# Two-layer graph attention with expert routing: pairwise routing, split slot search and early weights in the change

## The chip, the cores and the metric

The kernel runs on one core of one Trainium2 chip. The metric is the device time of one execution in microseconds (us), as the median of several runs. Below, PE is the matrix engine (TensorE), DVE the vector engine (VectorE), ACT the scalar engine (ScalarE), POOL is GpSimd, and SP is the engine whose queue issues most transfers between memory (HBM) and the on-chip SBUF. PSUM is the memory that matrix products land in.

## What is computed

`x` has 2708 rows of 256 float32 numbers and `adj` is a 2708 x 2708 matrix of zeros and ones. Two layers follow each other. Each one adds a graph attention to `x` and then a mixture of experts:

```python
x = x + _L0_gnn_ref(_layernorm(x), adj, L0_gnn_W, L0_gnn_a)
x = x + _L0_ffn_ref(_layernorm(x)[None], Wg, bg, W1, b1, W2, b2)[0]       # 8 experts, 256 -> 1024 -> 256, gelu
x = x + _L1_gnn_ref(_layernorm(x), adj, 1, W_gcn, W_att, a_att)
x = x + _L1_ffn_ref(_layernorm(x)[None], gate_w, gate_b, w1, b1, w2, b2, gamma, beta)[0]  # 16 experts, 256 -> 512 -> 256, relu
```

In both mixtures a row picks the two experts with the highest gate logits. The softmax over these two logits gives their weights. The output of an expert is `act(x @ W1[e] + b1[e]) @ W2[e] + b2[e]`, and a row's result is the weighted sum of its two experts. The second mixture adds its input and normalises the sum with `gamma` and `beta`.

## The kernel before

The 2708 rows are 22 tiles of 128 rows (the last holds 20), one row per SBUF partition. Instructions are written in program order. A scheduling layer then sets the order on each engine, and each engine works through its own list strictly in that order, waiting at an instruction whose input is not there yet. The stages follow one another, and only their edges overlap:

1. **Attention 0** (the loop over `pairs` of two tiles, 0 to 333 us). For each pair, `weigh` (ACT L722, DVE L725) makes the scores against each of the 22 tiles and `gather` (PE L735) sums them up. The work that `beside` lists is spread between: for the pair before, the layer norm, `Router.turn` (writes the rows to memory as `rows_d`, transposes them) and `Router.gate` (PE L341, DVE L364: the logits).
2. **Routing 0** (start of `experts`, L404 onward). From the logits of all tiles at once, DVE finds the two experts of each row as a one-hot tile `hot` (L429 to L441). Matrix products with a triangle of ones and with ones (L451, L455) count how many rows before each row have the same expert. A scan (L461) adds up over the tiles. Every (row, choice) gets a slot in the list sorted by expert. The slots are cut into blocks of 128 that belong to one expert each (at most NB = 50 blocks in layer 0, 58 in layer 1). Then the list is inverted: for each of 44 groups (22 tiles, 2 choices) the tile `in_block` (L523) says which place in a block a row takes and `which` (L513 to L518) says in which block, and the product of the two (L525) leaves the row's number at its place. This gives `comes` (which row to fetch) and `goes` (where to write the result). `whose` is the expert of a block. Biases are spread over blocks (L555). The weighted `b2` is added to every tile (the loop with L567 transpose, L569 copy, L571 product, L572 add). Only then does `gates_scope.close()` give the memory to the pool that holds the expert weights.
3. **Experts 0** (the loop over 50 blocks). SP loads 1 MB of W1 (L584) and 1 MB of W2 (L586) per block, with three buffers each. POOL gathers 128 rows (L589). PE transposes them (L336), computes the hidden part (L601, with ACT L603 behind it) and the output of the block before (L611). DVE copies it out (L614) and POOL scatters it into `outs_d` (L615).
4. **Combine 0 with projection 1** (`ready1`, then L640 onward). `ready1` loads the weights of the second attention (W_gcn, W_att, a_att) into a pool of its own on the freed memory, and multiplies them into `w1x` (L846, L852). Then each tile's two results are read back as `two` (L640), weighted and added (DVE L645), normalised and multiplied by `w1x` (PE L341 into `u_ps`).
5. **Scalar mathematics and attention 1** (about 840 to 1063 us).
6. **Layer norm and routing 1** (about 1063 to 1165 us): the loop over `groups` of four tiles makes `y_all` (L326), transposes it and makes the logits; then the code of point 2 runs with 16 experts.
7. **Experts 1** (58 blocks, 0.5 MB of each weight per block) and **combine 1** with the last norm (DVE, 1390 us to the end).

Of the kernel before, what the change touches and what calls it, by code (L numbers as in the profile page):

```python
# [9 lines left out]
F32 = mybir.dt.float32  # L10
# [5 lines left out]
I32 = mybir.dt.int32  # L16
# [16 lines left out]
def kernel(  # L33
# [152 lines left out]
    b2_1 = const.tile([E1, D], F32, name="b2_1")  # L186
    nc.gpsimd.dma_start(b2_1, L1_ffn_b2)
    gamma = broadcast_rows("gamma", L1_ffn_gamma, 0, D)
    beta = broadcast_rows("beta", L1_ffn_beta, 0, D)
# [155 lines left out]

    class Router:


        def __init__(self, layer, E, w_gate, b_gate):
            self.w_gate, self.b_gate, self.E = w_gate, b_gate, E  # L350
            self.rows_d = dram.tile([N, D], F32, name=f"rows_d{layer}")
            self.logits = sm.tile([P, T, E], F32, name=f"logits{layer}")
            nc.gpsimd.memset(self.logits, 0.0)
            self.xt = {}
# [11 lines left out]


# [4 lines left out]
    def blocks_of(E):  # L372
        return (2 * N - E) // P + E

    tri = const.tile([P, P], BF16, name="tri")
    nc.gpsimd.memset(tri, 1.0)
    nc.gpsimd.affine_select(out=tri, in_=tri, pattern=[[1, P]], compare_op=OP.is_gt,
                            fill=0.0, base=0, channel_multiplier=-1)
    ones_bf = const.tile([P, P], BF16, name="ones_bf")
    nc.gpsimd.memset(ones_bf, 1.0)  # L380
    iota_p = const.tile([P, P], F32, name="iota_p")
    nc.gpsimd.iota(iota_p, pattern=[[1, P]], base=0, channel_multiplier=0,
                   allow_small_or_imprecise_dtypes=True)
    own = const.tile([P, 1], F32, name="own")
    nc.gpsimd.iota(own, pattern=[[0, 1]], base=0, channel_multiplier=1,
                   allow_small_or_imprecise_dtypes=True)
    pair_no = const.tile([P, 2], F32, name="pair_no")
    nc.gpsimd.iota(pair_no, pattern=[[1, 2]], base=1, channel_multiplier=2,
                   allow_small_or_imprecise_dtypes=True)
    tile_of = const.tile([P, 2 * T], BF16, name="tile_of")  # L390
    nc.gpsimd.iota(tile_of, pattern=[[0, 2], [1, T]], base=0, channel_multiplier=0,
                   allow_small_or_imprecise_dtypes=True)
    valid = const.tile([P, T], F32, name="valid")
    nc.gpsimd.memset(valid, 1.0)
    nc.gpsimd.affine_select(out=valid, in_=valid, pattern=[[-P, T]], compare_op=OP.is_gt,
                            fill=0.0, base=N, channel_multiplier=-1)
    nowhere = const.tile([P, T], F32, name="nowhere")
    nc.gpsimd.memset(nowhere, 0.0)
    nc.gpsimd.affine_select(out=nowhere, in_=nowhere, pattern=[[-P, T]], compare_op=OP.is_gt,
                            fill=1e6, base=N, channel_multiplier=-1)  # L400

    def experts(layer, router, b1_rows, w1, w2, b2, func, acc_all, ready, done):
# [7 lines left out]
        plan = scope.enter_context(tc.tile_pool(name=f"plan{layer}", bufs=1))  # L410
        gates_scope = ExitStack()
        gates = gates_scope.enter_context(tc.tile_pool(name=f"gates{layer}", bufs=1))
        rows_d, logits = router.rows_d, router.logits
        outs_d = dram.tile([2 * N + NB * P, D], F32, name=f"outs_d{layer}")


        def per_token(v):
            return v.unsqueeze(2).to_broadcast([P, T, E])

        def tmp(name, dtype=F32):  # L420
            return gates.tile([P, T, E], dtype, name=f"{name}{layer}")

        rank_b = rank[E].unsqueeze(1).to_broadcast([P, T, E])
        hot = gates.tile([P, 2, T, E], BF16, name=f"hot{layer}")
        top = []
        rest = logits
        for k in range(2):
# [653 lines left out]
```

## Time and profile before

The median of three runs is 1458.44 us (1457.97 to 1460.83). The profiled execution spans 1457.3 us.

| engine | busy us | share of the span | instructions |
|---|---|---|---|
| PE | 1184.7 | 81% | 7294 |
| DVE | 589.2 | 40% | 1905 |
| ACT | 681.4 | 47% | 1632 |
| POOL | 236.4 | 16% | 297 |

PE is the engine with most work, and in the two attentions and in the two expert loops it is busy without a gap. A share of busy time is an average, though. In the stages between them PE waits, and its granted clock (PEclk, a share of full speed) falls to a half. The stages show in a table of busy time in stretches of 20 us. Each line of that table begins with the stretch, then has its length, then for PE, the weight loads of PE (PEld), DVE, ACT and POOL the busy time and, after an x, the number of instructions, then PEclk, the mean busy share of the transfer engines and the GB/s they moved. In a timeline, a line is a start time, a length, the engine, the source line, the operation with its output and inputs, a count where several were merged, and in square brackets how long the engine had been idle and what ended the wait.

### The profile page before, as it was taken

What the parts mean: (1) busy time and instruction counts of PE and PEld (TensorE: products, weight loads), DVE (VectorE), ACT (ScalarE), POOL (GpSimd) and SP (SyncE); (2) the same over time, 40 slices, a digit from 0 to 9 for tenths busy, and PEclk for the clock granted to TensorE, in tenths of its full rate; (3) what the DMA queues carried; (4) which work ended last, traced back from release to release, by engine and by line L of the source; (5) the groups of instructions that cost most, each with busy time, mean ns of one, the idle gap of its engine ahead of it and who ended that gap; (6) DMA issues with size and microseconds to landing.
All of it is one profiled execution on the core that took longest, in us unless ns stands there. A gap on an engine that the chain in (4) does not pass through costs nothing. (4 is left out here: it accounts for less than half of the span.)

```text
span 1457.3 us, 21300 instructions
## 1 busy us (share of the span) xinstructions
PE 1184.7 (81%) x7294; PEld 1002.1 (69%) x7294; DVE 589.2 (40%) x1905; ACT 681.4 (47%) x1632; POOL 236.4 (16%) x297
## 2 busy tenths in 40 slices
PE   3999999993899999999992929997052999999910
PEld 2778888852599999999991408996051599999810
DVE  4756566637300000000004765566468501111179
ACT  3877777741144444444431546664611144444400
POOL 4000000000022222222211100000000045555400
PEclk9999999996599999999996969998555599999965
DMA  7313333000299999999963200000010199999943
GB/s 263 144 46 129 122 130 122 21 8 5 76 344 323 328 327 326 327 327 327 327 216 109 65 0 1 1 1 1 0 58 19 37 319 354 353 352 342 327 143 98
DMA packets 145181, 248.46 MB, mean 170 GB/s; under 512 B 9351, under 2 KB 102302, under 8 KB 142366
## 3 DMA queue, kind: packets, MB, share of 16 engines
q1 hardware_dynamic: 134354, 218.39, 43.3%
q0 software_dynamic: 10720, 28.72, 6.3%
q8 instruction: 58, 0.95, 0.3%
q14 instruction: 49, 0.40, 0.1%
HBM read 224.60 MB, written 22.47 MB: 170 GB/s over the span
## 5 line engine op out<-in xcount | busy, mean ns | idle before, releaser
L601 PEld LDWEIGHTS hid_ps<-xg_t,w_b 128*128 128x128 f32 x2528 | 301.3, 194 | 10.9 <-ACT xg_t L337 4.7
L611 PE MATMUL out_ps<-w_b,ht 128*128 128x256 f32 x1264 | 308.1, 380 | 0.0
L601 PE MATMUL hid_ps<-xg_t,w_b 128*128 128x128 f32 x2528 | 304.2, 277 | 1.8 <-ACT xg_t L337 1.0
L603 ACT ACTIVATE ht<-hid_ps,bias 128x128 f32<-128x128 f32 x632 | 232.2, 368 | 149.6 <-PE hid_ps L601 114.9
L614 DVE COPY yo<-out_ps 128x256 f32<-128x256 f32 x108 | 45.9, 425 | 548.2 <-PE out_ps L611 548.2
L735 PE MATMUL att_ps<-g_all,z 128*128 128x257 f32 x968 | 245.8, 391 | 0.6 <-DVE z L725 0.6
L611 PEld LDWEIGHTS out_ps<-w_b,ht 128*128 128x128 f32 x1264 | 224.3, 191 | 22.0 <-issue 0.2
L735 PEld LDWEIGHTS att_ps<-g_all,z 128*128 128x128 f32 x968 | 165.2, 185 | 42.6 <-issue 13.5
L589 POOL DMA_INDIRECT xg<-rows_d,comes x108 | 104.5, 967 | 477.8 <-PE tr_ps L336 314.6
L722 ACT ACTIVATE zr<-e_bc,minus_one,g_all 128x256 f32<-128x256 f32 (+1 forms) x242 | 139.9, 590 | 53.8 <-DVE z L725 52.0
L725 DVE SCALAR_TENSOR_TENSOR z<-zr,mask_t 128x256 f32<-128x256 f32 (+1 forms) x242 | 99.2, 410 | 92.5 <-PE att_ps L735 79.2
L946 PE MATMUL att_ps<-half,wide_mask 128*128 128x258 f32 x968 | 124.2, 287 | 0.0
L946 PEld LDWEIGHTS att_ps<-half,wide_mask 128*128 128x128 f32 x968 | 118.3, 188 | 6.2 <-issue 0.4
L615 POOL DMA_INDIRECT outs_d<-yo,goes x108 | 106.7, 988 | 71.4 <-issue 36.9
L337 ACT COPY xg_t<-tr_ps 128x256 f32<-128x256 f32 x108 | 40.2, 372 | 166.4 <-PE tr_ps L336 166.3
L468 POOL MEMSET edge<- 128x9 f32 (+1 forms) x2 | 0.2, 111 | 530.5 <-PE att_ps L735 314.0
L938 ACT CAST wide_mask<-mask_t 128x1408 fp32r<-128x1408 fp8e4 x44 | 59.9, 1368 | 45.2 <-PE att_ps L946 45.2
L712 ACT CAST mask_t<-mt_ps 128x1024 fp8e4<-128x1024 bf16 (+2 forms) x66 | 57.1, 871 | 24.4 <-PE mt_ps L709 24.2
L336 PE MATMUL tr_ps<-ident,y_all 128*128 128x128 f32 (+1 forms) x44 | 13.2, 426 | 62.9 <-DVE y_all L326 62.8
L709 PE MATMUL mt_ps<-ident_bf,mb 128*128 128x128 bf16 (+1 forms) x484 | 42.2, 226 | 17.8 <-DVE mb L700 16.8
L709 PEld LDWEIGHTS <-mb 128*128 128x128 bf16 (+1 forms) x484 | 34.3, 102 | 29.8 <-DVE mb L700 17.7
L336 PEld LDWEIGHTS tr_ps<-ident,y_all 128*128 128x128 f32 (+1 forms) x44 | 8.9, 251 | 63.8 <-DVE y_all L326 58.0
(288 smaller groups left out, 1179.3 us busy)
## 6 DMA issues: line engine op xcount, KB each, us to landing
w_b<-in_L_ffn_W_dram SPq DMA_DIRECT2D x100, 1024.0 KB, 9.3
w_b<-in_L_ffn_w_dram SPq DMA_DIRECT2D x116, 512.0 KB, 6.3
ad<-in_adj_dram SPq DMA_DIRECT2D x21, 1354.0 KB, 5.8
two<-outs_d SPq DMA_DIRECT2D x42, 256.0 KB, 2.9
rows_d<-xn SPq DMA_DIRECT2D x21, 128.0 KB, 1.7
rows_d<-y_all SPq DMA_DIRECT2D x21, 128.0 KB, 1.7
out_dram<-xn SPq DMA_DIRECT2D x21, 128.0 KB, 1.7
xg<-rows_d,comes POOLq DMA_INDIRECT x108, 6.1
```

Of the source, the lines that this page charges most:

```text
L589: nc.gpsimd.indirect_dma_start(out=xg, out_offset=None, in_=rows_d[:, :], in_offset=bass.IndirectOffsetOnAxis(ap=comes[:, b:b + 1], axis=0))
L601: nc.tensor.matmul(ps[:, :P], w1_b[:, c, f * P:(f + 1) * P], xt[:, c, :], start=(c == 0), stop=(c == DC - 1))
L603: nc.scalar.activation(ht[:, f, :], ps[:, :P], func, bias=bias[:, f, b:b + 1])
L611: nc.tensor.matmul(ps[:, :D], ht[:, f, :], w2_b[:, f, :], start=(f == 0), stop=(f == FC - 1))
L615: ins = nc.gpsimd.indirect_dma_start(out=outs_d[:, :], in_=yo, in_offset=None, out_offset=bass.IndirectOffsetOnAxis(ap=goes[:, b:b + 1], a ...
L709: nc.tensor.transpose(ps[:w, k, :r], mbs[i][:r, c * P:c * P + w], ident_bf[:r, :r])
L712: nc.scalar.copy(mask_t[:, lo:lo + full, i * P:i * P + r], ps[:, :full, :r], saturate=False)
L722: nc.scalar.activation(zr[:k, :n], e_bc[:k, lo:lo + n], AF.Relu, bias=minus_one[:k], scale=g_all[:k, j, D + 1:D + 2])
L725: nc.vector.scalar_tensor_tensor(z[:k, :n], zr[:k, :n], 1.0, mask_t[:k, j, lo:lo + n], op0=OP.add, op1=OP.mult)
L735: nc.tensor.matmul(accs[i][:r, :D + 1], z[:k, q * P:q * P + r], g_all[:k, j, :D + 1], start=(j == 0), stop=(j == TF))
L938: nc.scalar.copy(m, mask_t[:, part * HALF:(part + 1) * HALF, i * P:(i + 1) * P])
L946: nc.tensor.matmul(accs[i][:, :D + 2], wide_masks[i, j // HALF][:k, j % HALF, :], half[:k, j, :], start=(j == 0 and half is halves[0]), st ...
```

## The change

It has five parts.

- **Routing pair by pair.** `Router` gets two methods. `pick` finds the two experts for a pair of tiles (DVE) and `number` counts their places (POOL adds the two choices, PE makes three small products, DVE adds a running `count`). In layer 0 they are put into attention 0 beside the next pair (`beside`, steps 16 and 20). In layer 1 they go into the loop of layer norm and logits, which now runs over pairs instead of groups of four.
- **Shorter slot search on two engines.** Slots no longer need the scan over tiles: a shift per expert is added to the place. `which` is made by POOL, one instruction for each of 44 groups, with the signed row number in it, so one column block replaces two; `in_block` is made by DVE, four groups per instruction. Both are now 4-byte tiles (float32r) with three buffers of four groups.
- **Weights with room of their own.** The pool for the expert weights is opened ahead of the routing's tiles and no longer shares their memory. `load` runs two blocks ahead in program order. In layer 0 the first buffer of `w1_b` holds the second attention's weights for the time of routing 0 (`load_weights`), and `combine_weights` makes `w1x` there instead of in `ready1`.
- **The b2 term spread over blocks.** Four tiles are done ahead of the block loop, the other 18 one per block.
- **Small things.** `outs_d` is laid out choice by choice, so `two` is read as two pieces of 1 KB per row. `gamma`, `beta` and the second `b2` are loaded after attention 1. Some constants go.

```diff
+        def pick(self, pair):
+            E, lo, n = self.E, pair[0][0], len(pair)
...
+            for k in range(2):
+                m = self.top[k]
+                nc.vector.tensor_reduce(m[:, lo:hi], seen, AX.X, OP.max)
+                at = row.tile([P, n, E], F32, name="at", tag=f"at{E}", bufs=2)
+                for q in range(n):
+                    nc.vector.scalar_tensor_tensor(at[:, q], seen[:, q], m[:, lo + q:lo + q + 1],
+                                                   rank[E], op0=OP.is_equal, op1=OP.mult)
+                first = row.tile([P, n], F32, name="first")
+                nc.vector.tensor_reduce(first, at, AX.X, OP.max)
...
+                nc.vector.tensor_tensor(self.hot[:, lo:hi, k], order,
+                                        first.unsqueeze(2).to_broadcast([P, n, E]), OP.is_equal)
...
+        def number(self, pair):
...
+            nc.gpsimd.tensor_tensor(both, self.hot[:, lo:hi, 0], self.hot[:, lo:hi, 1], OP.add)
...
+            nc.tensor.matmul(ps, tri, self.hot[:, lo:hi], start=True, stop=False)
+            nc.tensor.matmul(ps[:, :, 1], ones_bf, self.hot[:, lo:hi, 0], start=False, stop=True)
+            nc.tensor.matmul(sums, ones_bf, both, start=True, stop=True)
+            for q in range(n):
+                nc.vector.tensor_tensor(at[:, q], ps[:, q],
+                                        self.count.unsqueeze(1).to_broadcast([P, 2, E]), OP.add)
+                nc.vector.tensor_tensor(self.count, self.count, sums[:, q], OP.add)
+            nc.vector.tensor_tensor(at, at, self.hot[:, lo:hi], OP.mult)
+            nc.vector.tensor_reduce(self.place[:, lo:hi], at, AX.X, OP.add)
...
     def experts(...):
+        pool = scope.enter_context(tc.tile_pool(name=f"experts{layer}", bufs=3))
+        early(pool)
...
+        for g0 in range(0, G, CH):
...
+            for q in range(CH):
+                nc.gpsimd.tensor_scalar(which[:, q], iota_b, block[:, g:g + 1], signs[:, g:g + 1],
+                                        op0=OP.is_equal, op1=OP.mult)
+            nc.vector.tensor_tensor(
+                in_block, iota_p.unsqueeze(1).to_broadcast([P, CH, P]),
+                place[:, g0:g0 + CH].unsqueeze(2).to_broadcast([P, CH, P]), OP.is_equal)
+            for q in range(CH):
+                nc.tensor.matmul(pair_ps[:, :NB], in_block[:, q], which[:, q],
+                                 start=(g0 + q == 0), stop=(g0 + q == G - 1))
...
-        gates_scope.close()
-        pool = scope.enter_context(tc.tile_pool(name=f"experts{layer}", bufs=3))
...
+        ahead = [load(b) for b in range(2)]
+        aside()
+        for t, r in tiles[:4]:
+            add_b2(t, r)
         late = None
         for b in range(NB):
-            w1_b, w2_b, xg = load(b)
+            if b + 2 < NB:
+                ahead.append(load(b + 2))
+            w1_b, w2_b, xg = ahead.pop(0)
             ht = hidden(b, w1_b, xg)
             if late is not None:
                 outputs(*late)
             late = (b, w2_b, ht)
+            if b + 4 < T:
+                add_b2(*tiles[b + 4])
...
-                ins = nc.sync.dma_start(two[:r], outs_d[2 * t * P:2 * (t * P + r), :].rearrange(
-                    "(p k) d -> p k d", k=2))
+                ins = nc.sync.dma_start(two[:r], outs_d[:2 * N, :].rearrange(
+                    "(k n) d -> n k d", k=2)[t * P:t * P + r])
...
+            todo.setdefault(16, []).append(lambda: router0.pick(old))
+            todo.setdefault(20, []).append(lambda: router0.number(old))
...
+    def load_weights(pool):
+        room = pool.tile([P, DC, 1024], F32, name="w1_b").rearrange("p c f -> p (c f)")
...
+        nc.gpsimd.memset(parts["w_gcn"], 0.0)
+        nc.sync.dma_start(parts["w_gcn"][1:P, 0, 1:], L1_gnn_W_gcn[0:P - 1, :])
+        nc.sync.dma_start(parts["w_gcn"][:, 1, 1:], L1_gnn_W_gcn[P - 1:D - 1, :])
+        nc.sync.dma_start(parts["att_x"][:, :, :D], L1_gnn_W_att.rearrange("(c p) f -> p c f", p=P))
+        nc.sync.dma_start(parts["a1_j"], ...)
+    def combine_weights():
...
+            nc.vector.scalar_tensor_tensor(junk, att_x[:, c, :D], 1.0, l1["a1_j"], op0=OP.mult,
+                                           op1=OP.mult, accum_out=att_x[:, c, D:])
...
     def ready1():
...
-            w_att = rows_in_chunks("w_att", L1_gnn_W_att, setup, nc.sync)
-            a1_j = broadcast_rows("a1_j", L1_gnn_a_att, D, D, nc.sync, setup)
...
-    for g in groups:
-        ln_stats(ln_f1, x_tile, g)
+    for pair in pairs:
+        ln_stats(ln_f1, x_tile, pair)
...
+        for tl in pair:
+            router1.gate(*tl)
+        if before is not None:
+            router1.number(before)
+        router1.pick(pair)
+        before = pair
```

## The prediction

> **What bounds the kernel now.** I read busy time by stretches of 20 us first, since shares over the span hide the stages.
>
> ```profile
> 340.00:360.00 20.00, 1.58 (x8) 0.99 (x9) 18.74 (x60) 2.12 (x4) 0.00 (x0) 0.50 0.00 0
> 360.00:380.00 20.00, 20.00 (x86) 12.29 (x86) 11.38 (x54) 3.91 (x17) 0.00 (x0) 0.50 0.00 1
> 380.00:400.00 20.00, 16.07 (x41) 9.13 (x40) 6.30 (x15) 3.15 (x13) 2.95 (x3) 0.50 0.37 123
> ...
> 640.00:660.00 20.00, 20.00 (x140) 18.71 (x139) 1.03 (x3) 9.23 (x26) 4.71 (x5) 1.00 0.98 338
> ...
> 760.00:780.00 20.00, 6.92 (x29) 5.49 (x28) 1.63 (x6) 0.65 (x2) 4.19 (x8) 0.74 0.15 46
> ...
> 1120.00:1140.00 20.00, 9.55 (x47) 6.60 (x48) 19.24 (x59) 1.81 (x8) 0.00 (x0) 0.50 0.00 0
> 1140.00:1160.00 20.00, 20.00 (x62) 11.80 (x62) 7.48 (x23) 3.54 (x14) 0.00 (x0) 0.50 0.00 1
> ```
>
> In the expert loop (640 us) PE is full at full clock. In both routings DVE is full first, then PE at half clock with nothing moved. At 760 us nearly all stand. The timelines of these three places show the hand-overs.
>
> ```profile
> 359.63 8.31 DVE L523 TENSOR_SCALAR in_block<-iota_p,place 128x128 bf16<-128x128 f32 x42
> ...
> 379.61 5.48 PE L571 MATMUL b_ps<-b,wt 8*128 8x256 f32 x12
> ...
> 392.99 1.05 POOL L589 DMA_INDIRECT xg<-rows_d,comes  x1 [59.46 <-PE b_ps L571]
> ...
> 400.50 5.62 PE L601 MATMUL hid_ps<-xg_t,w_b 128*128 128x128 f32 x32 [0.51 <-ACT xg_t L337]
> ```
>
> The gather's input was ready at 375.6 (L537), yet it waited until 393 for the last b2 products, since its buffer shares memory with the routing's tiles.
>
> ```profile
> 768.21 0.38 SPq L115 DMA_DIRECT2D w_att<-in_L_gnn_W_att_dram  x1
> ...
> 770.66 0.60 SPq L107 DMA_DIRECT2D a_j<-in_L_gnn_a_att_dram  x1
> ...
> 778.29 0.42 DVE L841 SCALAR_TENSOR_TENSOR junk<-w_att,a_j 128x256 f32<-128x256 f32 x1 [13.12 <-DMA a_j<-in_L_gnn_a_att_dram]
> ...
> 782.77 27.41 SPq L640 DMA_DIRECT2D two<-outs_d  x19
> ```
>
> Layer 1's weights take 10.1 us from first issue to last use, and the read-back `two` queues behind their products.
>
> ```profile
> 1101.89 0.41 DVE L364 TENSOR_TENSOR logits<-gate_ps,bg 128x16 f32<-128x16 f32 x2 [1.66 <-PE gate_ps L341]
> ...
> 1124.00 2.82 DVE L513 TENSOR_TENSOR which<-iota_p,place 128x2552 bf16<-128x2552 f32 x1
> ...
> 1161.48 1.01 POOL L589 DMA_INDIRECT xg<-rows_d,comes  x1 [98.23 <-PE wt_ps L567]
> ...
> 1167.48 3.78 PE L601 MATMUL hid_ps<-xg_t,w_b 128*128 128x128 f32 x16 [0.51 <-ACT xg_t L337]
> ```
>
> **What the Trainium skill says.** "GPSIMD Engine Reference", section 3.1, has GpSimd at about half the Vector engine's speed for two-input element work. Its section 1 says the two share SBUF interfaces, with contention when a Vector instruction has two SBUF inputs, as `in_block` has. The trace has POOL copies only: 185 ns median for 128x1 (L864) but 504 at most while DVE works, 398 for 128x255. "TensorE: Matmul & The Clock Gate", "What's actually happening", has PE at half clock after an idle window; the trace agrees (0.50 at 340 to 400). "DMA: Bandwidth & Descriptors", "Specifications", asks 512 bytes for line rate, so 1 KB pieces of `two` should do; 1 KB rows of `rows_d` land in 1.7 us.
>
> **The change, part by part.** Times are on the clock of the kernel before.
>
> *Attention 0.* Ten pairs gain three small bf16 products each, about 0.1 us per product with its weight load (L525: 12 in 1.21): 10 x 0.3 = **+3 us**, as PE is full. Some 19 small DVE operations per pair fit in: DVE is busy 161 of 270 us between 60 and 330. In the build's order `hot` stands before a z that waits on PE, about three z ahead of the product that needs it, so PE shouldn't wait.
>
> *Routing 0.* Attention ends at 332.7; logits were done at 339.4. In the order of the changed program, the DVE operation that needs `a1_j` stands ahead of the last logits, and these weights can only start when attention ends, as their buffer is its memory. Queued behind it is all of DVE's routing. By the 10.1 us above it runs at 342.8, so logits come at 343.6. The last `pick` is 13 dependent operations at 0.2 us (L318 to L322 follow at that pace): 346.2. `number`: POOL add and PE 0.7, DVE 6 x 0.2: 348.1. Block counts 6 x 0.2, `moved` and its sum 0.5 each, four small ones 0.8, and `beyond` with its sum 1.1 in between: 352.2. Then the pair products. POOL: 44 of 50 numbers. The low bound is 0.2 (a one-input copy), the high one 0.5 (the slowest copy); I take 0.3, so 13.2 us. PE at half clock: 44 x 0.22 (a 4-byte weight load, as gate's x8 in 1.76) plus 8 biases at 0.55 and 1.8 of w1: 16 us. DVE: 11 x 0.6. PE is last: 368.5. `comes` 0.8, gather 7.3 (1.0 to issue as at 392.99, and 6.3 until the rows are there, 399.3), transpose and copy 1.2: first hidden product at 377.8, not 400.5: **-22.7 us**. The rest of w1 and four b2 terms (7 us) hide behind the gather; weights of blocks 0 and 1 leave at 353 and land ahead of it.
>
> *Expert loops.* 18 b2 terms lie in each. On PE: a transpose 0.11, two passes of 0.217 (L611: 4 in 0.87): 0.55. The product also waits for ACT's copy of `wt` (0.26 plus hand-overs); two row transposes (0.22) cover some, so 0.25 stays. PE was full, so 18 x 0.8 = **+14.4 us**, twice. In layer 1 transfers are as full (352 GB/s), but buffers hold three blocks only, so slack gained early isn't kept.
>
> *Combine 0.* `two` starts when the last rows are scattered, 768.3, not 782.77: **-14.4 us**. From there DVE is full as before.
>
> *Layer norm and routing 1.* Before, 11 pairs took 1066 to 1102, with PE and DVE taking turns. Now DVE has per pair four large operations (0.33) and 28 small ones, 0.08 us apart when independent and 0.2 when dependent. At 0.11 that is 4.4 us a pair, and about one more waits for gate: 50 us in all would end at 1116 (**+14**). The tail: `pick` and `number` of the last pair 4.8, counts 1.2, `moved` and its sum 1.8, `beyond` and its sum 2.2, small ones 0.7: `which` starts at 1126.7. Pairs: POOL 44 x 0.3 = 13.2, PE 9.7 plus 4 biases and a b2 term: 14.3. So 1141.0; `comes` 0.8, gather 4.8 (1161.48 to 1166.3), transpose and copy 1.2: 1147.8, not 1167.5: **-19.7 us**, the +14 included.
>
> *Nothing:* constants, `gamma`, `beta` (loaded at 1063, used at 1390), scalar mathematics, the last combine, which is DVE's own.
>
> Sum: 3 - 22.7 + 14.4 - 14.4 - 19.7 + 14.4 = **-25.0**: 1458.4 - 25.0 = 1433.4, say **1434 us**.
>
> **Rivals.**
> (1) *Cheap POOL, b2 hidden.* POOL at 0.2, PE warm at full clock in the pair products (5 us less per routing), and b2 at its bare 0.55 (9 less over both loops): -19, **1415 us**. For it: PE has work through the routing. Against: at 360 to 380 PE was busy 20 of 20 us at clock 0.50.
> (2) *POOL becomes the bound.* At 0.55 us, held up by DVE's two-input operations, 44 take 24.2 us: 8 more than PE in layer 0, 10 in layer 1: **1452 us**. For it: 504 ns copies beside DVE. Against: DVE needs only 6.6 us of these 24.
> (3) *Slower.* As (2), and the small DVE operations of the layer-1 loop all at 0.2: 28 x 0.2 + 1.3 = 6.9, with waits 8 us a pair, 88 us instead of 50: 1452 + 38 = **1490 us**. For it: each waits on another of DVE's. Against: the order interleaves independent chains.
>
> **How the numbers follow.** Forecast 0.56, (1) 0.18, (2) 0.20, (3) 0.06. Cases 1 and 2 bound POOL's cost and b2's; between them lies 1415 to 1452, and I reach 1 and 2 us past them, leaving out (3) and the outer halves of the cases: 1414 to 1454. Faster by over 0.2% (under 1455.5): all but (3) and a little of (2): 0.91; within: 0.03; slower: 0.06.
>
> **What would show it.** First hidden product of layer 0 some 45 us after attention's end (68 before); DVE waiting about 4 us for `a_j` ahead of the last logits; a `which` of 0.3 us; 0.8 us more per block for 18 blocks; `two` right after the last scatter; the layer-1 loop at about 4.5 us a pair. Wrong it would be if `which` takes over 0.5 us, if rank products hold up attention, or if that loop takes 8 us a pair.

## The result, and the profile after

The changed kernel takes 1472.19 us as the median of four runs (1469.68 to 1476.06), the kernel before 1458.78 us beside it. The ratio is 1.0092 with a 95% interval of 1.0067 to 1.0117: the change made the kernel 0.9% slower. The profiled execution spans 1469.9 us after and 1457.3 us before, 12.6 us apart.

The forecast was 25 us the other way. To find where the 37.6 us between the two went, I cut both traces at the same events. Each row is the time from one event to the next.

| stretch, from ... to ... | before | after | change | forecast |
|---|---|---|---|---|
| start to first product of attention 0 | 39.2 | 36.0 | -3.2 | 0 |
| attention 0, first to last product | 293.6 | 294.5 | +0.9 | +3 |
| last product to first `which`, layer 0 | 20.9 | 19.7 | -1.2 | -1.4 |
| slot search (first `which` to the copy of its sum), layer 0 | 20.6 | 29.2 | **+8.6** | -4.3 |
| that copy to first hidden product, layer 0 | 26.2 | 6.8 | -19.4 | -16.9 |
| experts 0, first hidden to end of last output product | 364.2 | 384.3 | **+20.1** | +14.4 |
| to the first combine operation | 20.8 | 6.9 | -13.9 | -14.4 |
| to the first product of attention 1 | 100.0 | 97.5 | -2.5 | 0 |
| attention 1 | 123.9 | 124.0 | +0.1 | 0 |
| its last product to first `which`, layer 1 | 114.6 | 124.1 | **+9.5** | +2.7 |
| slot search, layer 1 | 19.2 | 30.6 | **+11.4** | -4.9 |
| to first hidden product, layer 1 | 24.3 | 5.1 | -19.2 | -17.5 |
| experts 1, first hidden to last output product | 221.2 | 241.8 | **+20.6** | +14.4 |
| to the end | 68.6 | 69.4 | +0.8 | 0 |

The forecast column splits the recorded steps at the same events: for instance a search of 352.2 to 368.5 is 16.3 us, 4.3 less than the 20.6 before. Two things were forecast well, the gap ahead of the combine and what leaves from behind the search. Three were not: both searches, the price of a `b2` term in the block loop, and the loop of layer 1.

The table of busy time in stretches of 20 us, for the changed kernel, with the columns as before:

```profile
340.00:360.00 20.00, 6.55 (x21) 4.87 (x20) 12.52 (x59) 0.62 (x3) 12.31 (x20) 0.50 0.37 137
360.00:380.00 20.00, 16.68 (x52) 13.30 (x52) 4.67 (x10) 1.95 (x8) 18.90 (x31) 0.50 0.20 74
...
400.00:420.00 20.00, 19.62 (x129) 16.86 (x128) 2.54 (x6) 8.73 (x25) 5.88 (x6) 1.00 0.78 260
...
1120.00:1140.00 20.00, 11.31 (x30) 8.32 (x30) 8.53 (x19) 0.83 (x4) 17.04 (x23) 0.50 0.47 159
```

In both routings the fifth busy column, POOL, has taken the place of DVE: 18.90 of 20 us from 360 on. DVE has only 4.67 us of work there. In the expert loop (400 us) PE is at 19.62, still full to the eye, but transfers fell to 260 GB/s from 343 in the same stretch of the kernel before: PE is busy with something else than the experts' weights.

The timeline of routing 0 of the changed kernel, and the answer for the line that makes `which` (duration in ns as least, median, most; then who waited for it, with us and times):

```profile
340.34 0.42 DVE L850 SCALAR_TENSOR_TENSOR junk<-w_b 128x256 f32<-128x256 f32 x1 [5.60 <-DMA w_b<-in_L_gnn_a_att_dram]
350.19 28.71 POOL L499 TENSOR_SCALAR which<-iota_p,block,signed 128x50 fp32r<-128x50 f32 x44 [2.07 <-DVE place_in L486]
350.37 1.88 DVE L501 TENSOR_TENSOR in_block<-iota_p,place_in 128x512 fp32r<-128x512 f32 x3
352.66 1.95 PE L505 MATMUL pair_ps<-which,in_block 128*128 128x50 f32 x4 [8.36 <-POOL which L499]
...
379.40 0.21 DVE L548 COPY token<-pair_ps 128x50 f32<-128x50 f32 x1 [5.98 <-PE pair_ps L505]
```

```profile
L499 POOL TENSOR_SCALAR which<-iota_p,block,signed x88: 528/558/2447, 350.2 to 1152.5; 128x50 fp32r<-128x50 f32 x44, 128x58 fp32r<-128x58 f32 x44
...
who waited for it (us, times):
  PEld pair_ps L505: 39.9, 69
```

POOL runs without a pause for 28.71 us, 0.65 us per `which`, where I had taken 0.3. Most of them start 0.52 us after the one before. The first of each layer took 2.42 and 2.45 us: in layer 0 it lies beside three `in_block` of DVE, 1.88 us long together. Later, each `which` that meets one `in_block` takes twice the usual time:

```profile
354.65 0.71 DVE L501 TENSOR_TENSOR in_block<-iota_p,place_in 128x512 fp32r<-128x512 f32 x1 [2.40 <-PE pair_ps L505]
354.65 1.04 POOL L499 TENSOR_SCALAR which<-iota_p,block,signed 128x50 fp32r<-128x50 f32 x1
```

Layer 0 has eight of these later meetings, and the `which` in them takes 1.04 to 1.08 us. PE's products wait for POOL.

The timeline of one block of experts 0 that carries a `b2` term (after); the next block begins at 425.14, so the period is 8.37 us, where a block without a term takes 7.25 (later in the same loop). In layer 1 the two are 4.91 and 3.73 us.

```profile
416.76 0.27 PE L567 MATMUL wt_ps<-ident,wts 128*8 128x128 f32 x1
416.87 0.38 PE L332 MATMUL tr_ps<-ident,xg 128*128 128x128 f32 x2
417.38 0.29 PEld L571 LDWEIGHTS b_ps<-b,wt 8*128 8x128 f32 x2 [0.36 <-ACT wt L569]
417.38 0.69 PE L571 MATMUL b_ps<-b,wt 8*128 8x256 f32 x2
418.01 3.84 PE L598 MATMUL hid_ps<-xg_t,w_b 128*128 128x128 f32 x32
421.68 3.62 PE L608 MATMUL out_ps<-w_b,ht 128*128 128x256 f32 x16
425.14 0.27 PE L567 MATMUL wt_ps<-ident,wts 128*8 128x128 f32 x1
```

The transpose of the gathered rows stands behind all output products, next to the term, and what ACT copies for both is waited for. In blocks without a term it stands between the output products, which hide its copy.

The gap ahead of the combine, after: the last output product ends at 770.55, and the read-back is issued as soon as the last rows are scattered.

```profile
771.28 0.97 POOL L612 DMA_INDIRECT outs_d<-yo,goes  x1 [2.49 <-DVE yo L611]
773.87 6.08 SPq L645 DMA_DIRECT2D two<-outs_d  x5
777.44 0.48 DVE L650 SCALAR_TENSOR_TENSOR x_all<-two,wf,x_all 128x256 f32<-128x256 f32 x1 [6.43 <-DMA two<-outs_d]
```

Layer 1 of the changed kernel, from the last logits to the first hidden product:

```profile
1110.09 0.16 DVE L388 TENSOR_TENSOR logits<-gate_ps,bg 20x16 f32<-20x16 f32 x1
...
1122.96 30.14 POOL L499 TENSOR_SCALAR which<-iota_p,block,signed 128x58 fp32r<-128x58 f32 x44 [3.55 <-DVE place_in L486]
...
1153.60 0.22 DVE L548 COPY token<-pair_ps 128x58 f32<-128x58 f32 x1 [6.03 <-PE pair_ps L505]
```

### The profile page after: what moved, and what is told of

The parts are those of the page before. It is cut to its first block, busy times and chain, and to the rows that moved or that the text cites. A ratio compares the mean times of both kernels' runs of the same rounds, so it can differ in the third digit from the quotient of the medians.

```text
span 1469.9 us, 21846 instructions
## 1 busy us (share of the span) xinstructions
PE 1201.4 (82%) x7352; PEld 1008.1 (69%) x7352; DVE 606.1 (41%) x2191; ACT 678.7 (46%) x1635; POOL 305.0 (21%) x409
## 4 chain that ended last, share of the span: by engine, by line
PE 57%; issue 15%; DVE 11%; POOL 7%; DMA 5%; ACT 4%; SPq 1%; POOLq 0%; ACTq 0%; DVEq 0%
PE att_ps L740 15%; PE hid_ps L598 11%; PE out_ps L608 10%; PE att_ps L961 8%; POOL which L499 4%; POOL outs_d L612 2%; PE u_ps L337 2%; PE tr_ps L332 2%; PE b_ps L571 2%; PE gate_ps L337 2%; PE mt_ps L714 2%; DMA w_b<-in_L_ffn_w_dram 2%; PE h_ps L337 1%; DMA ad<-in_adj_dram 1%; DVE stat L229 1%
## 5 line engine op out<-in xcount | busy, mean ns | idle before, releaser
L598 PEld LDWEIGHTS hid_ps<-xg_t,w_b 128*128 128x128 f32 x2528 | 298.2, 193 | 21.2 <-ACT xg_t L333 15.2
L598 PE MATMUL hid_ps<-xg_t,w_b 128*128 128x128 f32 x2528 | 307.3, 278 | 2.5 <-DMA w_b<-in_L_ffn_w_dram 1.5
L600 ACT ACTIVATE ht<-hid_ps,bias 128x128 f32<-128x128 f32 x632 | 228.5, 367 | 166.0 <-PE hid_ps L598 69.8
L608 PE MATMUL out_ps<-w_b,ht 128*128 128x256 f32 x1264 | 302.0, 379 | 0.0
L420 POOL TENSOR_TENSOR both<-hot 128x16 bf16<-128x16 bf16 (+1 forms) x22 | 6.9, 314 | 368.9 <-DVE hot L408 310.6
L332 PE MATMUL tr_ps<-ident,y_all 128*128 128x128 f32 (+1 forms) x44 | 12.9, 427 | 69.4 <-DVE y_all L322 63.0
L505 PE MATMUL pair_ps<-which,in_block 128*128 128x50 f32 (+1 forms) x88 | 35.5, 414 | 30.6 <-POOL which L499 24.7
L499 POOL TENSOR_SCALAR which<-iota_p,block,signed 128x50 fp32r<-128x50 f32 (+1 forms) x88 | 58.8, 686 | 5.6 <-DVE place_in L486 5.6
```

Source lines behind the costliest of these rows:

```text
L499: nc.gpsimd.tensor_scalar(which[:, q], iota_b, block[:, g:g + 1], signs[:, g:g + 1], op0=OP.is_equal, op1=OP.mult)
L598: nc.tensor.matmul(ps[:, :P], w1_b[:, c, f * P:(f + 1) * P], xt[:, c, :], start=(c == 0), stop=(c == DC - 1))
L600: nc.scalar.activation(ht[:, f, :], ps[:, :P], func, bias=bias[:, f, b:b + 1])
L608: nc.tensor.matmul(ps[:, :D], ht[:, f, :], w2_b[:, f, :], start=(f == 0), stop=(f == FC - 1))
```

## The experiments

All start from the changed kernel unless they say otherwise, and all compute the whole result. "The stretch" and "the search" are those of the table above. Times are medians, ratios are to the kernel before on the same chip.

### 1. The slot search: who sets its pace

**`which` on DVE.**

```diff
-                nc.gpsimd.tensor_scalar(which[:, q], iota_b, block[:, g:g + 1], signs[:, g:g + 1],
+                nc.vector.tensor_scalar(which[:, q], iota_b, block[:, g:g + 1], signs[:, g:g + 1],
```

> The changed kernel with one word changed: which is made by DVE, not by POOL. In the changed kernel the slot search (first which to the copy of its sum) took 29.1 us in layer 0 and 30.6 us in layer 1, 0.65 us per which. Theory A (POOL's pace is the bound): the search falls to what PE needs for 44 products at half clock, 0.41 us each, with the biases 20 to 22 us, so about 8 to 9 us less in each layer: 1455 us. Rival B (PE's 4-byte products with their weight loads are the bound, POOL only looks like it since both run at the same pace): the search stays above 26 us, the time above 1466 us. Rival C (small f32 DVE operations of 0.2 us each, 44 of them beside 11 in_block of 0.7 us, make DVE the new bound): 17 us or less for DVE, so no worse than A.

Measured: 1454.71 us, ratio 0.9958 (0.9944 to 0.9971). One word turns the loss into a gain. The search takes 17.3 us in layer 0 and 17.5 us in layer 1 instead of 29.2 and 30.6. Its timeline:

```profile
351.70 0.94 DVE L499 TENSOR_SCALAR which<-iota_p,block,signed 128x50 fp32r<-128x50 f32 x4
352.57 0.67 DVE L501 TENSOR_TENSOR in_block<-iota_p,place_in 128x512 fp32r<-128x512 f32 x1
...
354.76 1.05 PE L505 MATMUL pair_ps<-which,in_block 128*128 128x50 f32 x4 [0.40 <-DVE in_block L501]
```

DVE makes four `which` in 0.94 us, 0.235 us each against POOL's 0.65, and four products fit into 1.05 us of PE. POOL's pace was the bound, as theory A has it. Theory A's price for PE was too high, though, and the new bound is DVE (rival C): the products wait 0.40 us per group of four for it. Not all of the 25 us came through: the time fell by 17.5 us. In layer 0 the stretch behind the search grew from 6.8 to 11.3 us, since the bias products (3.65 us of PE), which PE had fitted in between while it waited for POOL, now follow the search. In layer 1 the same stretch grew by 2.5 us and the block loop from 241.8 to 247.1 us. The first two blocks of that loop are 2.3 us longer; the rest lies in single late blocks, and the profiled run is the slowest of its ten, 3.6 us over their median.

**`in_block` with one tensor input.** This leaves POOL its work and takes away what may disturb it.

```diff
-            nc.vector.tensor_tensor(
-                in_block, iota_p.unsqueeze(1).to_broadcast([P, CH, P]),
-                place[:, g0:g0 + CH].unsqueeze(2).to_broadcast([P, CH, P]), OP.is_equal)
+            for q in range(CH):
+                nc.vector.tensor_scalar(in_block[:, q], iota_p, place[:, g0 + q:g0 + q + 1], None,
+                                        op0=OP.is_equal)
```

> The changed kernel with in_block made by four DVE operations with one tensor input each, not by one operation with two tensor inputs for four groups; which stays on POOL. In the changed kernel the first which, 2.4 us, lay beside three in_block of DVE, and the later ones came at 0.52 us when DVE was idle, 0.65 us on the mean. Theory A (POOL stands still while DVE runs an operation with two tensor inputs): the search falls from 29.1 and 30.6 us to 44 x 0.52 = 23 to 24 us, about 11 us in both layers, 1461 us. Rival B (the long first which is a start-up cost of POOL, or contention is with any DVE work): the search stays at 28 us or more, 1470 us.

Measured: 1464.91 us, ratio 1.0032 (1.0025 to 1.0040). The searches take 25.1 and 26.2 us, 4 us less each. The answer for the line of `which`:

```profile
L499 POOL TENSOR_SCALAR which<-iota_p,block,signed x88: 530/562/909, 350.8 to 1143.4; 128x50 fp32r<-128x50 f32 x44, 128x58 fp32r<-128x58 f32 x44
```

The median is as it was (562 against 558 ns), but the longest fell from 2447 to 909 ns. So POOL's price has two parts: about 0.52 us for the operation itself, and standing still while DVE runs an operation with two tensor inputs. The Trainium skill, "SBUF — State Buffer", "Who interferes with whom", describes an exclusive lock on the ports that the two engines share, and names this pair: a DVE instruction with two SBUF inputs contends with a GpSimd instruction that reads SBUF. The trace agrees: 2.42 us for the `which` that met 1.88 us of `in_block`, 1.04 to 1.08 for those that met 0.70 to 0.74 us, against 0.53 alone. Of POOL's 28.7 us in layer 0, 22.7 are the first part (44 x 0.515) and 6.0 the second. With one-input operations 1.9 us of the second part are left (the `which` beside them still take up to 0.91 us), so theory A's 23 to 24 us was not quite reached and the time came out between the two theories.

**The search in bf16 on DVE.** The row number is split in two, as in the kernel before, and DVE makes 3 operations per group.

```diff
-            which = gates.tile([P, CH, NB], F32R, name="which", bufs=3)
+            which = gates.tile([P, CH, 2, NB], BF16, name="which", bufs=3)
...
+                for c in range(2):
+                    nc.vector.tensor_scalar(which[:, q, c], iota_bf[:, :NB], block[:, g:g + 1],
+                                            halves_no[:, c, g:g + 1], op0=OP.is_equal, op1=OP.mult)
+                nc.vector.tensor_scalar(in_block[:, q], iota_bf, place[:, g:g + 1], None,
+                                        op0=OP.is_equal)
```

> The changed kernel with the search in bf16 on DVE alone: the row number is split in tile number and row in the tile, so which has two column blocks again, as in the kernel before, and a product costs what a bf16 product costs (about 0.1 us). DVE makes 3 small operations per group, 132 in all. Theory A (POOL's pace set the search): with 0.1 us per operation 13 us of DVE work, search 14 to 16 us instead of 29.1 and 30.6, time about 1443 us. Rival B (DVE's small operations come at 0.2 us, as 42 in_block of the kernel before did in 8.31 us): search 26 us, time about 1465 us.

Measured: 1471.36 us, ratio 1.0080 (1.0052 to 1.0108): nothing gained. The searches take 25.4 and 25.7 us, 3.8 and 4.9 less, but behind them 4.3 and 2.5 us come back, much as in the first run. Rival B is right about the search: a bf16 `which` of 50 numbers follows the one before after 0.21 us, a 4-byte one after 0.22, and the 3 operations per group take 0.57 us. The count of DVE operations decides here, not the products.

### 2. The b2 term

**All terms ahead of the loop.**

```diff
-        for t, r in tiles[:4]:
+        for t, r in tiles:
             add_b2(t, r)
...
-            if b + 4 < T:
-                add_b2(*tiles[b + 4])
```

> The changed kernel with all 22 b2 terms ahead of the block loop, none in it. In the changed kernel the first four terms took 3.3 us ahead of the loop in layer 0 (PE at half clock), 0.83 us each, while a term in the loop costs 1.13 us (layer 0) and 1.17 us (layer 1). Theory A (spreading the terms hid nothing, since PE is full in the loop, and made each dearer): the loops fall by 20.3 and 21 us, the first hidden product comes 18 x 0.83 = 15 us later in each layer, less up to 2 us that the gather hides: about 11 us gained in all, 1461 us. Rival B (terms at half clock with waits for ACT cost as much or more than in the loop, as in the kernel before): no gain or a loss, 1470 to 1480 us.

Measured: 1473.83 us, ratio 1.0095 (1.0075 to 1.0116). The loops fall by 19.8 and 20.9 us, to what the kernel before has (364.5 and 220.9 us), and the first hidden product comes 21.8 and 20.0 us later behind the search. Spread or not, 18 terms cost 1.1 to 1.2 us each: rival B.

**The term cut in two**: `add_b2` keeps the transpose and its copy, one block ahead; a new `sum_b2` has the product and the sum.

```diff
         for t, r in tiles[:4]:
             add_b2(t, r)
+            sum_b2(t, r)
+        add_b2(*tiles[4])
...
+            if b + 5 < T:
+                add_b2(*tiles[b + 5])
...
             if b + 4 < T:
-                add_b2(*tiles[b + 4])
+                sum_b2(*tiles[b + 4])
```

> The changed kernel with the b2 term of a tile cut in two: transpose and ACT copy one block ahead, the product a block later. The work on PE is the same; the wait for ACT's copy goes, and in the build's order the transpose of the gathered rows goes back between the output products. A block with a b2 term took 8.37 us in layer 0 (7.24 without) and 4.91 us in layer 1 (3.74 without). Theory A (0.55 us of this 1.13 and 1.17 is PE's own work, the rest waits for copies): a block with a term falls to about 7.8 and 4.3 us, 36 x 0.6 = 21 us in all, time about 1450 us. Rival B (all of the 1.13 us is PE's own time or DVE's sum, or layer 1's transfers bound the loop as soon as PE is faster): less than 8 us gained, time above 1463 us.

Measured: 1463.71 us, ratio 1.0020 (1.0011 to 1.0028). The loops take 380.1 and 238.1 us, 4.2 and 3.7 us less. Blocks with a term take 8.13 and 4.62 us instead of 8.37 and 4.91, so a term still costs 0.88 us. The whole gain is 8.5 us, close to rival B's limit of 8 and far from theory A's 21: most of the term was not the copies. Its timeline:

```profile
411.96 0.29 PEld L577 LDWEIGHTS b_ps<-b,wt 8*128 8x128 f32 x2 [0.33 <-issue]
411.97 0.69 PE L577 MATMUL b_ps<-b,wt 8*128 8x256 f32 x2
412.59 0.20 PEld L332 LDWEIGHTS tr_ps<-ident,xg 128*128 128x128 f32 x2 [0.33 <-ACT wt L571]
```

The weight load of the 8-row product and the next load behind it each stand 0.33 us. Nothing that the first waits for is named. The loads for the output products elsewhere in the loop stand 0.03 us.

**The same with 128 rows.** b2 and the transposed weights are padded with zero rows.

```diff
-    b2_0 = l0_pool.tile([E0, D], F32, name="b2_0")
+    b2_0 = l0_pool.tile([P, D], F32, name="b2_0")
+    nc.gpsimd.memset(b2_0, 0.0)
...
-            wt = row.tile([E, P], F32, name=f"wt{layer}")
+            wt = wt_room[:, t % 3]
```

> As the run before with the b2 term cut in two, and the product now has all 128 rows of the array: b2 is padded with zero rows and so are the transposed weights. In that run a block with a term still took 8.14 us in layer 0 and 4.62 us in layer 1, 0.9 us more than one without, of which 0.55 us are matrix passes. The weight load of the 8-row product stood 0.33 us without a releaser, and so did the next load after it. Theory A (the change between 8 or 16 rows and 128 rows empties PE's pipeline, twice per term): the gaps go, a block with a term takes about 7.8 and 4.3 us, and the time is about 12 us under the run before, 1451 us. Rival B (the gaps belong to the PSUM bank or to the queue, whatever the number of rows): 8.1 and 4.6 us stay, the time 1460 to 1465 us.

Measured: 1447.77 us, ratio 0.9917 (0.9893 to 0.9941), 16 us under the run with 8 rows. The loops take 372.1 and 227.9 us. Blocks with a term take 7.79 and 4.28 us, 0.34 us less than with 8 or 16 rows, so a term costs 0.54 and 0.55 us. That is 11.6 us over 34 such blocks; the rest lies in the first block of each layer and ahead of the loops. The product's load no longer stands:

```profile
413.54 0.30 PEld L580 LDWEIGHTS b_ps<-b,wt_room 128*128 128x128 f32 x2
413.65 0.60 PE L580 MATMUL b_ps<-b,wt_room 128*128 128x256 f32 x2
```

Eight and sixteen times the rows take less time. The edit also gives the transposed weights three places instead of two, but the 8-row product had waited for none that the trace names. Theory A holds as far as the gaps go with the row count; that a pipeline is emptied is my reading and not shown.

### 3. Pair by pair or at once

**Layer 1 at once after its loop**, with the code of the kernel before.

```diff
-        if before is not None:
-            router1.number(before)
-        router1.pick(pair)
...
+    router1.at_once()
```

> The changed kernel with the choice and the counting of layer 1 done for all tiles at once after its loop, as in the kernel before, loop over groups of four; layer 0 stays pair by pair, the search stays as changed. From the last product of attention 1 to the first which the changed kernel took 124.1 us, the kernel before 114.6 us. Theory A (the 28 small operations per pair keep DVE and PE taking turns and cost more in the loop than they save behind it): that stretch falls by about 9 us, time about 1462 us. Rival B (the loop over pairs is slow for another reason, such as groups of two in the layer norm alone): part of it stays when choice and counting leave, or the stretch is no shorter because the later tail grows: 1468 to 1475 us.

Measured: 1463.69 us, ratio 1.0018 (1.0008 to 1.0029), 8.5 us less. The stretch from attention 1 to the first `which` is 114.7 us, as before the change (114.6), not 124.1. Theory A's number came. The run also takes back the groups of four, so what of the 9.5 us belongs to the small operations and what to the loop over pairs (rival B) is not separated.

**Layer 0 at once after attention.**

```diff
-            todo.setdefault(16, []).append(lambda: router0.pick(old))
-            todo.setdefault(20, []).append(lambda: router0.number(old))
...
+    router0.at_once()
```

> The changed kernel with the choice and counting of layer 0 done for all tiles at once after attention 0, as in the kernel before; layer 1 stays pair by pair. In this build the product of W_att and a_j stands after the slot search on DVE, so that wait leaves too. From the last product of attention 0 to the first which it took 20.9 us before and 19.7 us after the change. Theory A (pair by pair beside attention saves only what is left after the wait for a_j, and costs 1 to 3 us of PE in attention): the stretch is 20 to 21 us again, attention 1 us shorter, time within 3 us of the changed kernel's 1472. Rival B (the work beside attention really left the path): 5 to 10 us slower, 1477 to 1482 us.

Measured: 1477.12 us, ratio 1.0114 (1.0093 to 1.0134). The stretch to the first `which` is 20.7 us (19.7 pair by pair) and attention 292.9 us (294.5), as theory A has it: the two cancel. The whole came out where rival B had it, but the other 4 us of its profile lie in stretches that the edit doesn't touch, the start (37.9 against 36.0 us) and the projection (100.2 against 97.5 us), and the interval overlaps that of the changed kernel. So the routing beside attention is worth nothing in this kernel as it stands. In this build DVE's wait for `a_j` ahead of the last logits is gone too; where pair by pair is freed of that wait (the first run of part 4), the stretch is 15.8 us, so without the wait the routing beside attention would save some 3 us (an estimate: 20.7 - 15.8, less 1.6 in attention).

### 4. The early weights

**Weights after the expert loop again.**

```diff
     def ready1():
         l0_scope.close()
+        with tc.tile_pool(name="setup1", bufs=1) as setup:
+            load_weights(setup)
+            combine_weights()
```

> The changed kernel with the weights of attention 1 loaded and combined after the expert loop again, in a pool of their own, as in the kernel before; nothing else is undone. The gap from the last expert product to the first combine operation was 20.8 us before and 6.9 us after the change. Theory A (the weights' 10 us from issue to last use, with the read-back queued behind them, made the gap): it goes back to about 20 us, +13.9 us, and in layer 0 DVE no longer waits for a_j ahead of the last logits (3.6 us between the end of the gate products and that operation), so the time is about 10 us above the changed kernel's 1472, 1482 us. Rival B (the layout of the results by choice, read in two pieces of 1 KB, or the earlier projection matters more): the gap stays under 15 us, less than 6 us in all.

Measured: 1477.14 us, ratio 1.0114 (1.0094 to 1.0134). The gap is 14.4 us, and the whole is 5.0 us slower: by its numbers this is rival B (under 15, less than 6). The early weights are worth 7.5 of the 13.9 us. The timeline shows the other 6.4:

```profile
774.05 8.89 SPq L645 DMA_DIRECT2D two<-outs_d  x4
...
780.78 0.42 DVE L850 SCALAR_TENSOR_TENSOR junk<-w_b 128x256 f32<-128x256 f32 x1 [13.12 <-POOL w1x L852]
...
781.56 0.48 DVE L650 SCALAR_TENSOR_TENSOR x_all<-two,wf,x_all 128x256 f32<-128x256 f32 x1
```

Here the read-backs leave at 774.05, ahead of the weights' product, where in the kernel before they stood behind it. What holds the combine is DVE's own order: the product of W_att and a_j stands ahead of the first combine operation. Which of the other edits freed the read-backs was not tried. And the early weights cost something where they now are: without them the stretch to the first `which` in layer 0 falls from 19.7 to 15.8 us, the 3.9 us that DVE waited for `a_j`, and the stretch behind the search from 6.8 to 5.0. The net gain of the early weights is so 7.5 - 5.7 = 1.8 us in these stretches. Most of the other 3 us lie in the start (38.7 against 36.0 us), which the edit doesn't touch.

### 5. A version that beats both

**All that helped together:** b2 with 128 rows and cut in two, layer 1 at once, and `which` on DVE in two operations per four groups.

```diff
+            nc.vector.tensor_tensor(
+                here, iota_b.unsqueeze(1).to_broadcast([P, CH, NB]),
+                block[:, g0:g0 + CH].unsqueeze(2).to_broadcast([P, CH, NB]), OP.is_equal)
+            nc.vector.tensor_tensor(
+                which, here, signs[:, g0:g0 + CH].unsqueeze(2).to_broadcast([P, CH, NB]), OP.mult)
```

> A version meant to beat both: which on DVE in two operations with two tensor inputs per four groups (0.27 us each expected), in place of four of 0.235 us; choice and counting of layer 1 at once after its loop; b2 terms cut in two and with 128 rows. Expected from the parts: which on DVE alone gained 17 us, two operations instead of four another 0.4 us x 11 in each layer = 9 us, layer 1 at once 8.5 us, b2 8.5 us as measured plus 12 us if the padding works: 1472 - 17 - 9 - 8.5 - 20.5 = 1417 us. If the padding does nothing: 1429 us. If two-input operations of 200 elements take over 0.45 us each: 9 us more.

Measured: 1416.20 us, ratio 0.9697 (0.9677 to 0.9718). The search of layer 0 takes 13.9 us, that of layer 1 17.6 us. The sum of the parts was met to 1 us, with some luck: the parts as measured alone (17.5, 8.5 and 24.4 us) make 1422 us, so the two operations, 0.35 us each and not 0.27, brought about 6 of the 9 us expected of them. They were not run alone.

**W_att and a_j in tiles of their own, loaded at the start.**

```diff
+    att_x = const.tile([P, DC, D + 1], F32, name="att_x")
+    nc.gpsimd.dma_start(att_x[:, :, :D], L1_gnn_W_att.rearrange("(c p) f -> p c f", p=P))
+    a1_j = broadcast_rows("a1_j", L1_gnn_a_att, D, D)
```

> The version that beat both, with W_att and a_j loaded at the start into tiles of their own, so that DVE's product of the two no longer waits for them ahead of layer 0's last logits. In the changed kernel DVE sat idle 5.6 us ahead of that product, and POOL and PE had nothing to wait for but it: the gate products end about 337 us, the product came at 340.3 us. Theory A (the wait is on the path, as the prediction said): about 3 us from the first stage of routing 0, 1413 us instead of 1416 us, unless the two loads at the start delay attention. Rival B (logits are late anyway): the same 1416 us.

Measured: 1419.90 us, ratio 0.9716 (0.9699 to 0.9732): no gain. The stretch from attention to the search does fall, from 19.6 to 15.9 us, but attention begins at 41.5 us instead of 37.5.

**The same, loaded behind the first rows of adj.**

```diff
+        if k == 4:
+            todo.setdefault(5, []).append(load_att)
```

> As the version with W_att and a_j in tiles of their own, but loaded behind the first rows of adj, so that DVE's product of the two comes among attention's work and not ahead of it. In that version the stretch from attention's last product to the first which fell from 20.4 to about 16.7 us, but attention began at 41.5 us in place of 37.5 us, since the product stood as tenth operation on DVE and waited for its loads. Theory A (both hold): attention starts at 37 to 38 us, the stretch stays at 16.7 us, 1412.5 us, 3.7 us under the version that beat both (1416.2 us, ratio 0.9697 to the kernel before; 0.967 expected). Rival B (the late start had another cause, such as another order of ACT's work): no gain.

Measured: 1409.58 us, ratio 0.9664 (0.9650 to 0.9677). Attention starts at 36.8 us, and the stretch stays at 15.8 us. The gain over the version that beat both is 6.6 us between the two medians and about 4.8 by the two ratios, where 3.7 was forecast; the reason forecast for the late start was wrong. In the run before, DVE's product had not waited for its two loads: the operation ahead of it, which turns the second tile of adj into a mask, had waited for adj, until 23.51 us. That is 7.1 us after the first such mask, against 5.8 in the version without these loads and 5.7 in this one. The timeline of that run:

```profile
23.51 1.57 DVE L794 TENSOR_SCALAR mb<-ad 128x2708 bf16<-128x2708 int32 x1 [3.07 <-DMA ad<-in_adj_dram]
25.16 0.39 DVE L935 SCALAR_TENSOR_TENSOR junk<-att_x,a_j 128x256 f32<-128x256 f32 x1
```

The later mask makes about 1.4 of the 4 us. The rest is order: in that build the norm statistics of the next tiles stand behind this mask in DVE's list, in the other two some of them stand ahead of it and fill the wait.

## Why the prediction was wrong, point by point

- **The two searches: 29.2 of the 37.6 us.** The step that failed is "I take 0.3" for `which` on POOL. It costs 0.52 us alone and 0.65 with the standstills, so POOL needs 28.7 and 30.1 us where I had PE as the last with 16.3 and 14.3. The sign that I had named, a `which` of over 0.5 us, is what came. Rival (2) named the mechanism, "POOL becomes the bound", and the evidence for it. It was mis-sized too: 0.55 us per `which` would give 24.2 us. Both ends of my price came from copies of one number per partition. The low end has nothing in it for 50 numbers and a second operation. The high end, 504 ns, is not a dear copy but a copy of 0.18 us that stood still: in that trace the copies that lie across DVE's L645, which has two tensor inputs, take 0.38 to 0.50 us (804.45), and those beside nothing or beside one-input statistics 0.18 (810.22). The kernel before thus showed the standstill. I set DVE's 6.6 us against it as small; they cost POOL 6.0 us, on top of a price that was too low by itself. ("Copies only" was a misreading as well: POOL also made selections of 0.30 to 0.40 us there, L377 and L395.) With the searches of the kernel before at 20.6 and 19.2 us, the change needed POOL at about 0.45 us or less to gain anything here.
- **The b2 term in the loop: 11.9 us.** "18 x 0.8" measured 18 x 1.12 and 18 x 1.14. The passes of 0.55 us were right (0.54 and 0.55 with 128 rows). The waits for copies, put at 0.25, measured about the same (8.37 - 8.13 = 0.24 in layer 0, 4.91 - 4.62 = 0.29 in layer 1). What I had at nothing is the price of a product with 8 or 16 rows among products with 128, 0.34 us per term.
- **The loop of layer 1: 6.8 us.** "50 us in all" (+14) measured +18.5 up to the last logits, 54.5 us or 4.95 a pair instead of 4.5, and the tail to the first `which` 12.9 us, not 10.7. Why a pair costs more is open, since the run that undid this part undid pairs and small operations together. The direction, and that the loop gives away what the tail saves, were right; with 124.1 instead of 117.3 us the part loses 9.5 us instead of 2.7.
- **Behind the search: 4.2 us better.** `comes`, gather, transpose and copy take 6.8 and 5.1 us, not 9.3 and 6.8.
- **Attention 0 and the start: 5.3 us better.** The rank products cost 0.9, not 3 us. And the start, which I didn't price, gained 3.2 in this profile: with `gamma`, `beta` and the second `b2` loaded later, the second tile of adj is worked on 5.7 us after the first, not 7.9. This was not run alone, and a part is chance: in eight other builds with the same loads at the start attention begins at 36.7 to 38.7 us, against 36.0 here. The pair of runs with W_att loaded at the start and later shows that loads there delay adj.
- **Right:** DVE's wait for `a_j` ahead of the last logits (its product at 9.8 us after attention's end, forecast 10.1), the first `which` of layer 0 (19.7 us after attention, forecast 19.5), and the gap ahead of the combine (-13.9, forecast -14.4). The gap was right in size partly by luck: only 7.5 us of it belong to the weights, which I had made the whole reason.
- **Left:** 2.5 us less in the projection and 1.3 us more at the gap and the end, which no run here explains; the projection took 95.7 to 100.2 us in builds that don't touch it.

The sum of these, 29.2 + 11.9 + 6.8 - 4.2 - 5.3 - 2.5 + 1.3, and 0.2 for the first `which`, is 37.4 us, within rounding the distance between forecast and profile. I gave "slower" a chance of 0.06, and only by way of rival (3), a layer-1 loop at 8 us a pair. Slower came without that, from a POOL dearer than rival (2) had it, a `b2` term that no case had above 0.8, and a loop at 4.95.

## What to carry to other kernels

Before work is moved to an idle engine, price one instruction of it there from a measured one of the same kind and size, and count how often the old engine's instructions will stop it. Here the idle engine was no gain, since each item cost it over twice as much and PE waited for every item. When a trace has one operation at two durations, look at what runs beside the slow ones before taking either as a price. Work spread into a loop is hidden only if the engine it needs has gaps in that loop: here PE had none, and the same terms cost the same ahead of it and in it. Compare a rewritten stage with its own time before the change, not with the sum of its parts after.

## What the runs showed of the hardware

- A `b2` term (a transpose and a product in two passes) costs 0.88 and 0.89 us in the block loops when the product has 8 or 16 rows, and 0.54 and 0.55 us when it is padded to 128 rows. The transpose, with 8 columns and 128 rows, stands in both versions and its own load shows no gap (0.03 us).
- POOL needs about 0.52 us from start to start for a compare-and-scale of 50 numbers per partition, DVE 0.22 us.
- POOL stands still beside a DVE operation with two tensor inputs: 1.04 to 1.08 instead of 0.53 us beside one of 0.70 to 0.74 us. With one-input operations 6.0 us of standstill became 1.9. It also goes the other way: in the version that beat both, an `in_block` of layer 1 took 1.41 instead of 0.68 us beside a sum of 1.05 us on POOL with two tensor inputs that had started first.
- On DVE 50 bf16 numbers cost about the same as 50 f32 numbers, 0.21 and 0.22 us from start to start, with two scalars per partition; one operation over 200 numbers with two tensor inputs takes 0.35 us.
